# Two-layer cross-attention: the output projections of three late units dealt out in halves

## Chip, cores, metric

The kernel runs on one NeuronCore of one Trainium2 chip. The metric is the device time of the program in microseconds (us). Each time shown is one execution, and the figure compared is the median over executions.

## What is computed

Two cross-attention layers are applied in turn to 32 samples of 256 tokens with 320 channels. Each sample attends to its own 77 context rows of 512 channels, with 20 heads of 16 channels. For the inputs given, both layers reduce to the same form (the image-prompt and object branches get no context rows), everything in float32:

```
q = x @ Wq ; k = ctx @ Wk ; v = ctx @ Wv          # 20 heads of 16
p = softmax(q k^T / 4)                            # over 77 context rows
x = x + (p v) @ Wo + bo                           # output projection and residual
...
# layer 0 with its weights, then layer 1 with its own on the result
```

## The kernel before, in words

**Units.** Samples are taken in pairs: 16 pairs, two layers, so 32 *units* `(pair, layer)`, listed by `units_in_order` (L81). The last five units are `(15,0)`, `(12,1)`, `(13,1)`, `(14,1)`, `(15,1)`, with numbers 27 to 31. Units 28 to 31 are all second-layer units of four different pairs, so none of them needs what another one writes. Their results only go to memory.

**Layout.** Activations lie with channels on the 128 partitions. A unit's x, q and o are tiles of 1280 columns: two blocks of 128 channels for the two samples (512 columns each), and the last 64 channels of both samples side by side (256 columns). This gives five *groups* g = 0..4 of 256 columns, each with four pairs of heads. `of_group` (L175) cuts one out. Group 2t+b is channel block t of sample b, and group 4 is the rest.

**Steps of one unit.** Each step is a Python function that issues instructions:

- `keys`, `keys_rest` (L215, L236), `queries`, `queries_rest` (L258, L270), `vals`, `place_vals` (L284, L302): the projections on TensorE (PE), copied out by ScalarE (ACT) or VectorE (DVE), with some DMAs on the SP queue.
- `maxima(u, g)` (L319): 16 matmuls into four PSUM tiles `psm`, and four row maxima on DVE (L334).
- `turn(u)` (L341): one DVE transpose of the unit's maxima into `mT` (L343), then eight small DMAs from SP (L347) that put the maxima into spare rows of the unit's q tiles. The first four go to q tile 0, the others to q tile 1. So a unit's `scores` can start only when these have landed.
- `scores(u, g)` (L353): 16 matmuls into four `pss` tiles (L360; eight with q tile 0, then eight with q tile 1), and four exponentials on ACT (L366).
- `values(u, g)` (L409): 16 matmuls into one tile `po` (`products`, L380); a DVE transpose (L392), a reciprocal (L396) and a multiplication on GpSimd, POOL (L401).
- `turn_back(u, g)` (L412): a DVE transpose (L415) into the unit's tile `oT`, which has two buffers (L371).
- `finish(u)` (L428): the output projection of groups 0 to 3. These are 96 matmuls at L173 into four `psy` tiles: 64 from the two channel blocks, then 32 from the last channels. Four DVE additions into x follow (L422).
- `finish_rest(u)` (L436): 24 matmuls (L212) and one addition for group 4, then the DMA that stores the pair's whole x (L443). The last unit stores each group by itself (L426).

**PSUM.** All matmul outputs come from one ring of eight tiles (`bank`, L103). The n-th tile asked for reuses the (n-8)-th, so it waits until that one has been read out.

**Order.** Nothing is scheduled by a tool: the order of the program is written out by *slots*. `at(slot, where, step)` files a step, and the loop at L497 to L501 issues, slot by slot, the steps in the order load, maxima, turn, scores, values, rest, back, full, last. Every engine and every DMA queue takes its instructions in that order. With s = 5u, a unit has its queries in slot s-9, maxima in s-6 to s-2, turn in s-2, scores in s to s+4, values and turn_back one slot later. Before the change, `finish` is in s+6 and `finish_rest` in s+8. Only the two last units differ: unit 30 has both in slot 159 and unit 31 both in slot 160, the last slot. So a full slot has maxima of unit u+1, scores and values of unit u, and some projections. The slots after 153 have no maxima and no projections of a later unit left.

In the last slots before the change, PE gets this besides scores and values:

| slot | before the change |
|---|---|
| 146 | maxima, finish(28), queries(31) |
| 147, 148, 149, 150 | maxima, and keys(31); finish_rest(28) and keys_rest(31); vals; queries_rest(31) |
| 151 | maxima(31,2), finish(29) |
| 152 | maxima(31,3) |
| 153 | maxima(31,4), turn(31), finish_rest(29) |
| 154 to 158 | nothing |
| 159 | finish(30), finish_rest(30) |
| 160 | values(31,4) alone, then finish(31), finish_rest(31) |

Scores run from (30,1) in slot 151 to (31,4) in slot 159, and values one slot behind, from (30,0) in slot 151 to (31,4) in slot 160.

Of the kernel before, what the change touches and what calls it, by code (L numbers as in the profile page):

```python
# [48 lines left out]
F32 = mybir.dt.float32  # L49
# [6 lines left out]
P = 128  # L56
NB = 2
NT = NB * S
NX = 2 * NT + S
NP = B // NB  # L60
NG = 5
# [19 lines left out]
def units_in_order():  # L81
    order = [(p, 0) for p in range(AHEAD)]
    for p in range(NP):
        order.append((p, 1))
        if p + AHEAD < NP:
            order.append((p + AHEAD, 0))
    return order
# [3 lines left out]
def xattn_kernel(ctx: ExitStack, tc: tile.TileContext, xT, cT, cP, weights, outT):  # L91
    nc = tc.nc
# [3 lines left out]
    work = ctx.enter_context(tc.tile_pool(name="work", bufs=3))  # L96
# [3 lines left out]
    units = units_in_order()  # L100
    NU = len(units)

    def bank(name):  # L103
        return psum.tile([P, 512], F32, tag="bank", name=name)

    xs, cs, cvs = {}, {}, {}

    def load_x(p):
        x_sb = io.tile([P, NX], F32, tag="x", name=f"x_{p}", bufs=AHEAD + 3)
        nc.sync.dma_start(out=x_sb, in_=xT[p])  # L110
        xs[p] = x_sb

    def load_context(u):
        p = units[u][0]
        c_sb = cs[u] = io.tile([P, NKA, NB * L], F32, tag="c", name=f"c_{u}", bufs=3)
        nc.sync.dma_start(out=c_sb, in_=cP[:, p])
# [51 lines left out]
    st = [{} for _ in units]  # L168

    def by_columns(out, lhsT, rhs, **flags):  # L170

        for m in range(0, out.shape[0], 32):
            nc.tensor.matmul(out[m : m + 32], lhsT[:, m : m + 32], rhs, **flags)  # L173

    def of_group(x, g):  # L175

        if g < 4:
            return x[:, (g // 2) * NT + (g % 2) * S : (g // 2) * NT + (g % 2 + 1) * S]
        return x[:, 2 * NT : NX]

    def last_channels(ps, w2, x, **flags):
        for t in range(2):
            for b in range(NB):
                r = slice(64 * b, 64 * b + 64)
                by_columns(
                    ps[t][b][:, 0:S], w2[r, 0, t * P : (t + 1) * P], x[r, 2 * NT : NX], **flags
                )

    def main_channels(ps, w, x, start, stop):
        for t in range(2):
            for kc in range(2):
                for b in range(NB):
                    i = kc * NT + b * S
                    by_columns(
                        ps[t][b][:, 0:S], w[:, kc, t * P : (t + 1) * P], x[:, i : i + S],
                        start=(start and kc == 0), stop=(stop and kc == 1),
                    )

    def project_rest(ps, w, w22, x):

        for kc in range(3):
            for i in range(4):
                b, m = i // 2, i % 2
                r = slice(32 * i, 32 * i + 32)
                if kc < 2:
                    lhsT = w[:, kc, 2 * P + 32 * m : 2 * P + 32 * m + 32]
                    rhs = x[:, kc * NT + b * S : kc * NT + (b + 1) * S]
                else:  # L210
                    lhsT, rhs = w22[:, 0, r], x[:, 2 * NT : NX]
                nc.tensor.matmul(ps[r, 0:S], lhsT, rhs, start=(kc == 0), stop=(kc == 2))  # L212


    def keys(u):  # L215
        p, layer = units[u]
        w, c_sb = w_sb[layer], cs[u]
        kT = st[u]["k"] = work.tile([P, 2, NG, L], F32, tag="kT", name=f"kT_{u}", bufs=3)
        for t in range(2):
            ps = bank(f"psk_{u}_{t}")  # L220
            for kc in range(NKA):
                by_columns(
                    ps[:, 0 : 2 * L],
                    w["k"][:, kc, t * P : (t + 1) * P],
                    c_sb[:, kc, :],
                    start=(kc == 0),
                    stop=(kc == NKA - 1),
                )
            nc.vector.tensor_tensor(
                kT[:, :, 2 * t : 2 * t + 2].rearrange("p e g k -> p e (g k)"),  # L230
                ps[:, 0 : 2 * L].unsqueeze(1).broadcast_to([P, 2, 2 * L]),
                masks.unsqueeze(2).broadcast_to([P, 2, 2 * L]),
                ALU.mult,
            )
# [44 lines left out]
    def load_chunk(layer, i):  # L279
        n = min(P, B * L - i * P)  # L280
        c_sb = cvs[layer, i] = io.tile([P, NKA, P], F32, tag="cv", name=f"cv_{layer}_{i}", bufs=3)
        nc.sync.dma_start(out=c_sb[:, :, :n], in_=cT[:, :, i * P : i * P + n])
# [85 lines left out]
    def products(u, g):  # L368
        vpad = st[u]["v"]
        if "o" not in st[u]:  # L370
            st[u]["o"] = work.tile([P, NX], F32, tag="oT", name=f"oT_{u}", bufs=2)  # L371
        po = bank(f"po_{u}_{g}")
        pT = st[u].pop(("p", g))
        for e in range(2):
            for j in range(4):
                if g < 4:
                    b, pair = g % 2, 4 * (g // 2) + j
                else:
                    b, pair = j // 2, 8 + j % 2
                nc.tensor.matmul(  # L380
                    po[32 * j : 32 * j + 32, e * S : (e + 1) * S],
                    vpad[:L, b, pair, e].rearrange("p a d -> p (a d)"),
                    pT[j][:L, e * S : (e + 1) * S],
                    start=True,
                    stop=True,
                )
        return po
# [30 lines left out]
    def add(u, g, ps):  # L418
        p, layer = units[u]
        x = of_group(xs[p], g)  # L420
        t = g // 2
        nc.vector.scalar_tensor_tensor(  # L422
            x, ps[:, 0:S], w_sb[layer]["b"][:, 0, t : t + 1], x, ALU.add, ALU.add
        )
        if u == NU - 1:
            nc.sync.dma_start(out=of_group(outT[p], g), in_=x)  # L426

    def finish(u):  # L428
        w = w_sb[units[u][1]]
        ps = [[bank(f"psy_{u}_{t}_{b}") for b in range(NB)] for t in range(2)]  # L430
        main_channels(ps, w["o"], st[u]["o"], start=True, stop=False)
        last_channels(ps, w["o2"], st[u]["o"], start=False, stop=True)
        for g in range(4):
            add(u, g, ps[g // 2][g % 2])

    def finish_rest(u):  # L436
        p, layer = units[u]
        w = w_sb[layer]
        ps = bank(f"psy_{u}_2")
        project_rest(ps, w["o"], w["o22"], st[u]["o"])  # L440
        add(u, 4, ps)
        if layer == 1 and u < NU - 1:
            nc.sync.dma_start(out=outT[p], in_=xs[p])  # L443
        st[u].clear()


    place = {}
# [1 line left out]
    def at(slot, where, step):  # L449
        place.setdefault((slot, where), []).append(step)  # L450

    made = [0, 0]
    for u, (p, layer) in enumerate(units):
        s = NG * u
        if layer == 0 and u > 0:
            at(s - 14, "load", lambda p=p: load_x(p))
        if u > 0:
            at(s - 12, "load", lambda u=u: load_context(u))
        at(s - 8 if u else s - 9, "rest", lambda u=u: keys(u))
        at(s - 9, "last", lambda u=u: queries(u))  # L460
        at(s - 7, "rest", lambda u=u: keys_rest(u))
        need = range(p * NB * L // P, ((p + 1) * NB * L - 1) // P + 1)
        when = s - 6
        for i in need:
            if i < made[layer]:
                at(when, "full", lambda u=u, i=i: place_vals(u, i))
                continue
            at(when - 3, "load", lambda layer=layer, i=i: load_chunk(layer, i))
            at(when, "full", lambda layer=layer, i=i: vals(layer, i))
            at(when, "full", lambda u=u, i=i: place_vals(u, i))  # L470
            made[layer] += 1
            when = s - 5
        at(s - 5, "rest", lambda u=u: queries_rest(u))
        for g in range(NG):
            at(s - 6 + g, "maxima", lambda u=u, g=g: maxima(u, g))
            at(s + g, "scores", lambda u=u, g=g: scores(u, g))
            at(s + g + 1, "values", lambda u=u, g=g: values(u, g))
            at(s + g + 1, "back", lambda u=u, g=g: turn_back(u, g))
        at(s - 2, "turn", lambda u=u: turn(u))
        if u < NU - 2:  # L480
            at(s + NG + 1, "full", lambda u=u: finish(u))
            at(s + NG + 3, "rest", lambda u=u: finish_rest(u))
        else:

            slot = NG * NU - (u == NU - 2)
            at(slot, "full", lambda u=u: finish(u))
            at(slot, "last", lambda u=u: finish_rest(u))


    at(-10, "load", lambda: load_weights(0, "v", "v", nc.scalar))  # L490
# [106 lines left out]
```

## Time and profile before

| | |
|---|---|
| runs shown | 992.94, 999.02, 1000.55 us |
| median of them | 999.02 us |
| the profiled execution: its own time | 995.15 us |
| its span, first to last instruction | 993.4 us |
| mean granted TensorE clock | 0.995 |
| busy in the span: PE, DVE, ACT, POOL | 977.5, 590.9, 421.7, 182.7 us |
| one maximum on DVE (L334), mean | 466 ns, x640 |
| one exponential on ACT (L366), mean | 590 ns, x640 |
| one addition on DVE (L422), mean | 479 ns, x160 |

All views are of the one profiled execution. A PE is called busy while matmuls are in flight, so a busy share says little of how fast it works. The granted clock is what the chip allowed TensorE, as a share of full speed. The chain of waits follows the work that ended last back from the end: each piece names what the end was waiting for at that time. Times are from the span's start. "L360" is a line of the kernel, and an entry such as `psy L173` is a tile name and a line.

### The profile page before, as it was taken

What the parts mean: (1) busy time and instruction counts of PE and PEld (TensorE: products, weight loads), DVE (VectorE), ACT (ScalarE), POOL (GpSimd) and SP (SyncE); (2) the same over time, 40 slices, a digit from 0 to 9 for tenths busy, and PEclk for the clock granted to TensorE, in tenths of its full rate; (3) what the DMA queues carried; (4) which work ended last, traced back from release to release, by engine and by line L of the source; (5) the groups of instructions that cost most, each with busy time, mean ns of one, the idle gap of its engine ahead of it and who ended that gap; (6) DMA issues with size and microseconds to landing.
All of it is one profiled execution on the core that took longest, in us unless ns stands there. A gap on an engine that the chain in (4) does not pass through costs nothing.

```text
span 993.4 us, 43878 instructions
## 1 busy us (share of the span) xinstructions
PE 977.5 (98%) x19664; PEld 609.0 (61%) x19664; DVE 590.9 (59%) x1380; ACT 421.7 (42%) x905; POOL 182.7 (18%) x236
## 2 busy tenths in 40 slices
PE   7899999999999999999999999999999999999988
PEld 4566665666666666665666666666666666666644
DVE  2466555666655665655666656666556656556654
ACT  1344343454444443444444444444444534444442
POOL 2122201221202222112222112221022221122211
PEclk9999999999999999999999999999999999999989
DMA  6541222221132411223212232311323111231111
GB/s 213 177 160 37 74 79 97 70 77 62 57 122 70 132 47 60 92 80 122 71 44 85 68 123 70 122 34 53 121 80 119 50 62 54 69 107 48 58 47 54
DMA packets 53949, 83.59 MB, mean 84 GB/s; under 512 B 15556, under 2 KB 35652, under 8 KB 53762
## 3 DMA queue, kind: packets, MB, share of 16 engines
q1 hardware_dynamic: 53330, 78.96, 23.9%
q8 instruction: 154, 2.52, 1.0%
q10 hardware_dynamic: 432, 1.84, 0.5%
q14 instruction: 33, 0.27, 0.1%
HBM read 35.39 MB, written 10.49 MB: 46 GB/s over the span
## 4 chain that ended last, share of the span: by engine, by line
PE 97%; DVE 1%; DMA 1%; SPq 1%; issue 0%; POOL 0%; DVEq 0%; POOLq 0%
PE po L380 16%; PE pss L360 15%; PE psy L173 14%; PE psq L173 14%; PE psm L326 12%; PE psv L173 8%; PE psk L173 7%; PE psq L212 4%; PE psy L212 4%; PE psk L245 2%; SPq L347 1%; DVE max L334 1%; DMA w<-in_w_dram 0%; DMA q<-mT 0%; DVE mT L343 0%
## 5 line engine op out<-in xcount | busy, mean ns | idle before, releaser
L366 ACT ACTIVATE pT<-pss 77x512 f32<-77x512 f32 x640 | 326.9, 590 | 242.1 <-PE pss L360 242.1
L334 DVE TENSOR_REDUCE max<-psm 128x4 f32<-128x308 f32 x640 | 259.4, 466 | 172.1 <-PE psm L326 172.1
L401 POOL TENSOR_TENSOR normal<-turned,inv 128x256 f32<-128x256 f32 x160 | 99.3, 621 | 763.9 <-DVE inv L396 763.9
L360 PE MATMUL pss<-q,kM 32*77 32x256 f32 x2560 | 180.6, 380 | 5.8 <-DMA q<-mT 5.8
L380 PE MATMUL po<-pT,v 77*32 77x256 f32 x2560 | 174.0, 389 | 1.0 <-DVE max L334 1.0
L173 PE MATMUL psy<-oT,w 128*32 128x256 f32 (+1 forms) x3072 | 149.4, 380 | 0.0
L173 PE MATMUL psq<-x,w 128*32 128x256 f32 (+1 forms) x3072 | 149.4, 380 | 0.0
L392 DVE STREAM_TRANSPOSE turned<-po 128x512 f32<-128x512 f32 x160 | 113.3, 708 | 46.0 <-PE po L380 42.9
L268 ACT COPY q<-psq 128x256 f32<-128x256 f32 x128 | 47.6, 372 | 213.3 <-PE psq L173 209.5
L326 PE MATMUL psm<-kT,q 32*128 32x154 f32 x2560 | 129.1, 314 | 0.0
L360 PEld LDWEIGHTS pss<-q,kM 32*77 32x77 f32 x2560 | 114.4, 142 | 23.4 <-issue 10.6
L326 PEld LDWEIGHTS psm<-kT,q 32*128 32x128 f32 x2560 | 91.9, 183 | 55.3 <-issue 41.7
L380 PEld LDWEIGHTS po<-pT,v 77*32 77x32 f32 x2560 | 67.5, 110 | 90.3 <-DVE max L334 58.4
L415 DVE STREAM_TRANSPOSE oT<-normal 128x256 f32<-128x256 f32 x160 | 70.9, 443 | 84.5 <-POOL normal L401 81.4
L173 PEld LDWEIGHTS psq<-x,w 128*32 128x32 f32 (+1 forms) x3072 | 85.4, 109 | 57.6 <-issue 14.4
L173 PEld LDWEIGHTS psy<-oT,w 128*32 128x32 f32 (+1 forms) x3072 | 82.2, 108 | 61.2 <-issue 13.2
L422 DVE SCALAR_TENSOR_TENSOR x<-psy,w,x 128x256 f32<-128x256 f32 x160 | 68.6, 479 | 62.8 <-PE psy L173 56.4
L173 PE MATMUL psv<-w,cv 128*32 128x320 f32 x1232 | 93.5, 433 | 0.0
L256 POOL TENSOR_SCALAR kM<-kT,less 128x385 f32<-128x385 f32 x64 | 79.9, 1260 | 38.8 <-ACT kT L253 38.6
L173 PE MATMUL psk<-c,w 128*32 128x154 f32 x2048 | 75.2, 299 | 5.6 <-DMA w<-in_w_dram 5.6
L173 PEld LDWEIGHTS psk<-c,w 128*32 128x32 f32 x2048 | 67.0, 112 | 12.8 <-DMA w<-in_w_dram 5.6
L173 PEld LDWEIGHTS psv<-w,cv 128*32 128x32 f32 x1232 | 41.0, 110 | 40.6 <-issue 1.9
(24 smaller groups left out, 328.3 us busy)
## 6 DMA issues: line engine op xcount, KB each, us to landing
q<-q SPq DMA_DIRECT2D x32, 640.0 KB
x<-in_xT_dram SPq DMA_DIRECT2D x16, 640.0 KB
c<-in_cP_dram SPq DMA_DIRECT2D x32, 308.0 KB
cv<-in_cT_dram SPq DMA_DIRECT2D x38, 256.0 KB
out_dram<-x SPq DMA_DIRECT2D x15, 640.0 KB
v<-stage SPq DMA_DIRECT2D x26, 192.5 KB
q<-mT SPq DMA_DIRECT2D x256, 5.0 KB
w<-in_w_dram ACTq DMA_DIRECT2D x2, 640.0 KB
```

The costliest lines, as they stand in the source:

```text
L173: nc.tensor.matmul(out[m : m + 32], lhsT[:, m : m + 32], rhs, **flags)
L212: nc.tensor.matmul(ps[r, 0:S], lhsT, rhs, start=(kc == 0), stop=(kc == 2))
L256: nc.gpsimd.tensor_scalar_add(kM[:, e], kT[:, e], less[:, e : e + 1])
L326: nc.tensor.matmul(ps[j][:, c * 2 * L : (c + 1) * 2 * L], q[r, c * P : (c + 1) * P], kT[r, :, g, :], start=True, stop=True,)
L334: nc.vector.tensor_reduce(mx[:, 2 * g : 2 * g + 2, 2 * j : 2 * j + 2], ps[j][:, : 4 * L].rearrange("p (c e k) -> p c e k", e=2, k=L), AX.X ...
L360: nc.tensor.matmul(ps[j][:L, e * S : (e + 1) * S], kM[r, e, g, :], q[r, :], start=True, stop=True,)
L366: nc.scalar.activation(st[u]["p", g][j][:L], ps[j][:L], AF.Exp, scale=SCALE)
L380: nc.tensor.matmul(po[32 * j : 32 * j + 32, e * S : (e + 1) * S], vpad[:L, b, pair, e].rearrange("p a d -> p (a d)"), pT[j][:L, e * S : (e ...
L392: nc.vector.transpose(turned[:, 0 : 2 * S], po)
L401: nc.gpsimd.tensor_tensor(normal.rearrange("p q e d -> p e q d"), outs, inv.unsqueeze(3).broadcast_to([P, 2, S // 32, HD]), ALU.mult,)
L415: nc.vector.transpose(of_group(st[u]["o"], g), normal)
L422: nc.vector.scalar_tensor_tensor(x, ps[:, 0:S], w_sb[layer]["b"][:, 0, t : t + 1], x, ALU.add, ALU.add)
```

## The change

Units 28, 29 and 30 (`late`) get their output projections placed by a table: the slots of the first half (channel block t = 0), of the second half (t = 1), and of `finish_rest`. With `end` = 160 these are 151, 152, 148 for unit 28; 153, 154, 155 for unit 29; and 156, 159, 157 for unit 30. `finish` can do one half: 48 matmuls into two `psy` tiles and two additions. The store becomes a step of its own, filed as the last step of the latest of the three slots: 152, 155 and 159. Unit 31 and all units up to 27 stay where they were. The tile `oT` gets a third buffer.

```
--- before.py
+++ after.py
@@ -180,16 +180,16 @@
 
 
 
-    def last_channels(ps, w2, x, **flags):
-        for t in range(2):
+    def last_channels(ps, w2, x, ts=(0, 1), **flags):
+        for t in ts:
             for b in range(NB):
                 r = slice(64 * b, 64 * b + 64)
                 by_columns(
                     ps[t][b][:, 0:S], w2[r, 0, t * P : (t + 1) * P], x[r, 2 * NT : NX], **flags
                 )
 
-    def main_channels(ps, w, x, start, stop):
-        for t in range(2):
+    def main_channels(ps, w, x, start, stop, ts=(0, 1)):
+        for t in ts:
             for kc in range(2):
                 for b in range(NB):
                     i = kc * NT + b * S
@@ -368,7 +368,7 @@
     def products(u, g):
         vpad = st[u]["v"]
         if "o" not in st[u]:
-            st[u]["o"] = work.tile([P, NX], F32, tag="oT", name=f"oT_{u}", bufs=2)
+            st[u]["o"] = work.tile([P, NX], F32, tag="oT", name=f"oT_{u}", bufs=3)
         po = bank(f"po_{u}_{g}")
         pT = st[u].pop(("p", g))
         for e in range(2):
@@ -425,13 +425,21 @@
         if u == NU - 1:
             nc.sync.dma_start(out=of_group(outT[p], g), in_=x)
 
-    def finish(u):
+    def finish(u, ts=(0, 1)):
+
         w = w_sb[units[u][1]]
-        ps = [[bank(f"psy_{u}_{t}_{b}") for b in range(NB)] for t in range(2)]
-        main_channels(ps, w["o"], st[u]["o"], start=True, stop=False)
-        last_channels(ps, w["o2"], st[u]["o"], start=False, stop=True)
-        for g in range(4):
-            add(u, g, ps[g // 2][g % 2])
+        ps = {t: [bank(f"psy_{u}_{t}_{b}") for b in range(NB)] for t in ts}
+        main_channels(ps, w["o"], st[u]["o"], start=True, stop=False, ts=ts)
+        last_channels(ps, w["o2"], st[u]["o"], start=False, stop=True, ts=ts)
+        for t in ts:
+            for b in range(NB):
+                add(u, 2 * t + b, ps[t][b])
+
+    def store(u):
+        p, layer = units[u]
+        if layer == 1 and u < NU - 1:
+            nc.sync.dma_start(out=outT[p], in_=xs[p])
+        st[u].clear()
 
     def finish_rest(u):
         p, layer = units[u]
@@ -439,9 +447,8 @@
         ps = bank(f"psy_{u}_2")
         project_rest(ps, w["o"], w["o22"], st[u]["o"])
         add(u, 4, ps)
-        if layer == 1 and u < NU - 1:
-            nc.sync.dma_start(out=outT[p], in_=xs[p])
-        st[u].clear()
+        if u not in late:
+            store(u)
 
 
     place = {}
@@ -449,6 +456,14 @@
     def at(slot, where, step):
         place.setdefault((slot, where), []).append(step)
 
+
+
+    end = NG * NU
+    late = {
+        NU - 4: (end - 9, end - 8, end - 12),
+        NU - 3: (end - 7, end - 6, end - 5),
+        NU - 2: (end - 4, end - 1, end - 3),
+    }
     made = [0, 0]
     for u, (p, layer) in enumerate(units):
         s = NG * u
@@ -477,14 +492,17 @@
             at(s + g + 1, "values", lambda u=u, g=g: values(u, g))
             at(s + g + 1, "back", lambda u=u, g=g: turn_back(u, g))
         at(s - 2, "turn", lambda u=u: turn(u))
-        if u < NU - 2:
+        if u == NU - 1:
+            at(s + NG, "full", lambda u=u: finish(u))
+            at(s + NG, "last", lambda u=u: finish_rest(u))
+            continue
+        at(late[u][2] if u in late else s + NG + 3, "rest", lambda u=u: finish_rest(u))
+        if u not in late:
             at(s + NG + 1, "full", lambda u=u: finish(u))
-            at(s + NG + 3, "rest", lambda u=u: finish_rest(u))
-        else:
-
-            slot = NG * NU - (u == NU - 2)
-            at(slot, "full", lambda u=u: finish(u))
-            at(slot, "last", lambda u=u: finish_rest(u))
+            continue
+        for t in range(2):
+            at(late[u][t], "full", lambda u=u, t=t: finish(u, (t,)))
+        at(max(late[u]), "last", lambda u=u: store(u))
 
 
     at(-10, "load", lambda: load_weights(0, "v", "v", nc.scalar))
```

## The prediction

> **What bounds the kernel now.** I read the page first, then the windows, the chain of waits, PE's waits, and the DVE timeline.
>
> ```profile
> PE 977.5 (98%) x19664; PEld 609.0 (61%) x19664; DVE 590.9 (59%) x1380; ACT 421.7 (42%) x905; POOL 182.7 (18%) x236
> PEclk9999999999999999999999999999999999999989
> ```
>
> PE is busy for 98% of the span, and the clock row falls in one place, the last slice but one. So nothing but PE matters in the middle, and the end has something of its own. The windows cut it out (columns: PE, PEld, DVE, ACT, POOL busy; clock; DMA share; GB/s):
>
> ```profile
> 58.00:944.00 886.00, 885.77 (x18006) 556.88 (x18004) 543.06 (x1267) 387.24 (x834) 166.71 (x208) 1.00 0.24 79
> 944.00:963.00 19.00, 15.49 (x265) 8.66 (x260) 11.25 (x27) 7.40 (x15) 2.48 (x4) 0.99 0.11 40
> 963.00:973.00 10.00, 10.00 (x88) 3.57 (x80) 2.83 (x6) 5.70 (x12) 1.24 (x2) 0.51 0.08 31
> 973.00:994.00 21.00, 17.02 (x324) 9.10 (x320) 9.71 (x22) 4.50 (x9) 2.48 (x4) 0.98 0.18 64
> ```
>
> From 58 to 944 us PE idles 0.23 us in all. From 944 to 963 it idles 3.5 us. Then for 10 us it is "busy" at half the clock: 88 matmuls, where 10 us in the middle hold about 203. The chain of waits (start, length, what) gives the pieces:
>
> ```profile
> 944.15 4.48 PE psy L173 x96
> 948.63 0.74 PE psm L326 x16
> 949.37 1.67 PE pss L360 x16
> 951.04 1.04 PE po L380 x16
> ...
> 955.91 0.52 DVE mT L343
> ...
> 960.65 1.66 DMA q<-mT
> 962.31 0.24 issue
> 962.55 1.15 PE pss L360 x8
> 963.70 1.87 PE po L380 x16
> 965.57 1.94 PE pss L360 x16
> ...
> 976.14 1.19 PE po L380 x16
> 977.33 4.48 PE psy L173 x96
> ```
>
> The first piece is finish(29), slot 151. The chain leaves PE in slot 153: the last maxima, the transpose mT, eight DMA issues, their landing at 962.31, and only then the second half of scores(31,0). Pieces of 0.86 (pss) and 1.00 (po) at full clock take 1.94 and 1.87 afterwards. PE's own waits confirm the gaps:
>
> ```profile
> PE pss L360 <- DMA q<-mT: 2.7, 2, 1.7
> PE po L380 <- DVE max L334: 0.8, 1, 0.8
> ```
>
> So the end is bound by two waits and a clock drop, with finish(30) (4.48 + 1.43 us) standing behind them where it covers nothing.
>
> **What the Trainium skill says.** "TensorE: Matmul & The Clock Gate", Part 1, says that TensorE's clock is either full or half, set by how busy the PE was in free-running windows of about 3.4 us, and that a busy window restores it. The trace agrees: 0.50 in the two-us windows from 964 to 972, 1.00 from 973, and the drop follows 2.7 us of idling within 959.2 to 962.6. "DMA: Bandwidth & Descriptors", Anatomy of one DMA, gives about 2 us of fixed cost per DMA; here the last 5 KB transfer landed 1.66 us after its issue. The same page, Queues, rings and completion order, says that each DMA engine consumes descriptors in ring order; nothing in this trace tests that for a store ahead of a turn.
>
> **The work at full speed.** The chain from 944.15 to the end of the last L212 matmuls at 990.06 lasts 45.91 us. At full-clock prices from the same chain its PE work is: finish(29) 4.48; maxima 2 x 0.74 = 1.48; scores (30,2) to (31,4), 8 x 0.86 = 6.88; values (30,1) to (31,4), 9 x 1.00 = 9.00; finish_rest(29) 1.30; finish and rest of 30 and of 31, 2 x 5.78 = 11.56. Sum 34.70. So 11.2 us are lost: idling 3.5 (0.81 + 0.98 + 1.72); half clock 5.4 (excess over full price of the six pieces from 962.55 to 973.07: 0.72 + 0.87 + 1.08 + 0.86 + 1.08 + 0.77); 0.8 in scores(30,2), which waited for finish(29)'s third and fourth additions to free PSUM tiles; the rest, 1.5, in small pieces.
>
> **The change part by part.**
>
> *Slot 146 loses finish(28): 4.48 us of PE earlier.* queries(31) then follows po at once, at 914.57. Its first PSUM tiles are psm tiles whose maxima end at 914.33, and one exponentiated by then: no wait. Its ACT copies came 2.4 us after its first matmul; the exponentials ahead of them end at 915.66, before 916.9. Slots 147 to 150 move up by 4.48; the chunk needed in slot 149 is issued at 913.27 and used at 935.5, so 17 us remain. Cost nothing.
>
> *The same matmuls come back in slots 151 and 152; no instruction is added.* 48 matmuls take 2.24 us, two additions about 0.42 each back to back (1.66 for four). Slots 151, 152, 153, 154, 156 and 159 get a half, 155 and 157 a rest of 1.30. Per slot PE then has 0.74 + 0.86 + 1.00 + 2.24 = 4.84 us to 153, 4.10 or 3.16 to 157, and 1.86 in 158. ACT needs 2.04 for four exponentials, so it is covered except in slot 158: values(31,3) follows its scores by 1.00 + 0.86 against 0.1 + 2.04, a wait of 0.3 (before, the same place cost 0.19).
>
> *DVE and the ring in slots 151 to 153.* DVE has four maxima 1.62, the transpose of po to the end of turn_back 2.3 (POOL in between), two additions 0.83: 4.75 of 4.84. In slot 152 scores take their third and fourth PSUM tiles from the two psy tiles of slot 151. With T the end of those matmuls, the additions end near T + 0.55 and T + 1.0, and the tiles are wanted at T + 0.96 and T + 1.07. That is a tie. Bounds: 0, or 0.81 as four additions cost before; I take 0.3 in slot 152 and 0.3 in 153.
>
> *turn(31).* With slot 151 starting at 937.07 (4.48 earlier), slot 153's maxima end on DVE at about 949.6 and mT at 950.1 (two additions are ahead of them, 0.8 us). Before, mT ended at 956.43 and the second half of scores(31,0) started 6.1 us later. So q tile 1 is ready at 956.2, q tile 0 about 2.4 earlier. PE's own work brings it to the second half at 956.2 without ring stalls and 956.8 with them: finish(29) in two halves is the cover, 4.48 us instead of a rest of 1.30. Margin 0 to 0.6 us; the wait of 2.7 and the clock drop behind it go. If the cover fails, each us late costs one us, and the clock is next.
>
> *Stores.* On SP, store(28) now stands ahead of the eight issues. It waits for its addition until about 948, takes 0.39 to issue, and a 640 KB store is done about 2.6 us after issue (store(29), issued 961.29; the DMA rate is 0 from 964). So it is gone near 951; the issues start at 950.1, and the last four near 952.5. Covered; at worst the first four land a us later, where q tile 0 has 2 us. store(29) in 155 and store(30) in 159 are behind all turns.
>
> *Third oT buffer.* oT of unit 30 first asks for a buffer in slot 151; with two it would be unit 28's, now read until 152. With three nothing waits. No instruction; no cost.
>
> *Tail.* Slot 160 and the output DMAs are as before.
>
> Sum: 11.2 recovered, less 0.6 (ring), 0.3 (slot 158), 0.2 (ends of L212 groups, 1.48 against 1.30): 10.1 us. The profiled execution's 995.15 becomes 985.0 (span 983.3). The three runs and it have the middle (995.15 + 999.02) / 2 = 997.1, which I take as the base: 997.1 - 10.1 = **987**.
>
> **Rivals.**
>
> *More ring stalls (0.18).* DVE at 4.75 of 4.84 us slips, and slots 152 to 154 each lose 0.81 instead of two losing 0.3: 1.8 more, 988.8. For it: scores(30,2) did so. Against: two additions, not four.
>
> *The turn is still late (0.10).* mT slips behind the additions, PE idles 2.7 and the clock halves as before (5.4): of 10.1, 2.0 is left, 995.1. Against: 3.2 us more cover.
>
> *The clock drop is not in the usual execution (0.10).* It hangs on a free-running window, and the lowest run is 2.2 below the profiled one. Then 10.1 - 5.4 = 4.7: 992.4. Against: that run is faster by less than the drop costs. The same doubt can help: 999.02 may hold a longer drop, and the gain would be up to 14.
>
> *Slower (0.02).* The store ahead of the turn holds its transfers: below about 0.6 us nothing is lost, then each us is one, and the clock's 5.4 returns. It passes 999.02 once the hold is over 0.6 + (999.0 - 987.0) - 5.4 = 7.2 us, and is 1% slower (1009) at 17 us; a store takes 2.6.
>
> **How the numbers follow.** The forecast has 0.60, with 983 to 991 as its own range, since the runs differ by 7.6 us. Lowest run less 10 to 14 is 979 to 983; the late turn and the missing drop reach 995 and 992. Range 979 to 994. One per cent, about what a measurement can tell here, is 10 us, so below 989.0 counts as faster against 999.02. Faster: 0.50 of the forecast, 0.10 of the ring case: 0.60. Same: 0.10 + 0.08 + 0.10 + 0.10 = 0.38. Slower 0.02.
>
> **What would show it.** Clock 1.00 in every window from 58 us to the end; PE's waits for q<-mT gone after 100 us; psy L173 in groups of 48; scores in slots 152 and 153 at 0.9 to 1.2 us; the last L212 ending near 980. A clock below 0.9 there, or a wait for q<-mT over 1 us, would make it wrong; so would idling between 914 and 937, where slot 146 lost its filler.

## The result, and the profile after

The changed kernel takes 987.82 us (median of 6 runs, 987.63 to 988.27), beside 995.13 us for the kernel before in the same comparison (6 runs, 992.84 to 1000.55). The ratio is 0.9913, with an interval of 0.9888 to 0.9937. A second comparison gave 988.07 against 997.36 us, ratio 0.9911 (0.9890 to 0.9931). The profiled execution took 987.73 us, with a span of 985.9 us, 7.5 us less than before.

The page of the kernel after, sections 1 and 2:

```profile
PE 973.4 (99%) x19664; PEld 608.9 (62%) x19664; DVE 591.6 (60%) x1380; ACT 421.7 (43%) x905; POOL 182.7 (19%) x236
PEclk9999999999999999999999999999999999999999
```

The instruction counts of all engines are those of before; only the order has changed. The one low digit in the clock row is gone. The windows of the kernel after (same columns as before):

```profile
944.00:963.00 19.00, 19.00 (x337) 10.05 (x338) 12.26 (x28) 8.64 (x17) 2.48 (x4) 1.00 0.12 43
963.00:973.00 10.00, 10.00 (x181) 5.09 (x174) 5.16 (x11) 6.40 (x14) 1.86 (x3) 1.00 0.15 60
```

From 944 to 963 us PE held 265 matmuls and 15.5 busy us before, and holds 337 and 19.0 now. From 963 to 973 it runs at clock 1.00, not 0.51, and does 181 instead of 88. PE has no idle time to speak of from 900 us to its last matmul at 982.6 (82.59 of 82.60 us busy). PE's waits over the whole span:

```profile
PE psk L173 <- DMA c<-in_cP_dram: 5.8, 1, 5.8
PE pss L360 <- DMA q<-mT: 3.1, 2, 1.6
PE po L380 <- DVE max L334: 0.2, 1, 0.2
```

The waits for the turn (`q<-mT`) were 5.8 us in four places. The two that are left lie in the first 41 us, outside the change. The chain of waits of the kernel after never leaves PE in its last 82 us:

```profile
940.65 2.32 PE psy L173 x48
942.97 0.74 PE psm L326 x16
943.71 1.32 PE pss L360 x16
945.03 1.00 PE po L380 x16
...
949.09 1.32 PE pss L360 x16
...
951.41 2.32 PE psy L173 x48
953.73 1.03 PE pss L360 x16
...
972.17 1.19 PE po L380 x16
973.36 2.32 PE psy L173 x48
975.68 1.00 PE po L380 x16
976.68 4.48 PE psy L173 x96
981.16 1.48 PE psy L212 x24
```

The pieces `x48` are halves; there are six of them, three of which are shown. (The trace shows a float32 matmul of the program as two records, so `x48` is 24 instructions; the counts of matmuls ahead of this section are counts of records.) Two things cost more than the prediction priced them at: the halves take 2.32 us, and scores take 1.32 in slots 152 and 153 and 1.03 in the slots without maxima.

### The profile page after: what moved, and what is told of

Same layout as the page of the kernel before. It is cut to its first block, busy times and chain, and to the rows that moved or that the text cites. A ratio compares the mean times of both kernels' runs of the same rounds, so it can differ in the third digit from the quotient of the medians.

```text
span 985.9 us, 43879 instructions
## 1 busy us (share of the span) xinstructions
PE 973.4 (99%) x19664; PEld 608.9 (62%) x19664; DVE 591.6 (60%) x1380; ACT 421.7 (43%) x905; POOL 182.7 (19%) x236
## 4 chain that ended last, share of the span: by engine, by line
PE 98%; DVE 1%; DMA 1%; SPq 0%; issue 0%; POOL 0%; POOLq 0%
PE po L380 16%; PE pss L360 15%; PE psq L173 15%; PE psy L173 15%; PE psm L326 12%; PE psv L173 9%; PE psk L173 7%; PE psq L212 4%; PE psy L212 4%; PE psk L245 2%; DMA c<-in_cP_dram 1%; SPq L347 0%; DVE max L334 0%; DMA q<-mT 0%; DVE mT L343 0%
## 5 line engine op out<-in xcount | busy, mean ns | idle before, releaser
L360 PE MATMUL pss<-q,kM 32*77 32x256 f32 x2560 | 177.9, 376 | 3.1 <-DMA q<-mT 3.1
L380 PE MATMUL po<-pT,v 77*32 77x256 f32 x2560 | 171.5, 385 | 0.2 <-DVE max L334 0.2
```

The source lines that it names most:

```text
L360: nc.tensor.matmul(ps[j][:L, e * S : (e + 1) * S], kM[r, e, g, :], q[r, :], start=True, stop=True,)
L380: nc.tensor.matmul(po[32 * j : 32 * j + 32, e * S : (e + 1) * S], vpad[:L, b, pair, e].rearrange("p a d -> p (a d)"), pT[j][:L, e * S : (e ...
```

## The experiments

My theory: idling before scores(31,0), while the turn's transfers are under way, takes the clock down. What pays is useful PE work behind the turn's transpose. Rivals: the thin slots 155 to 158 take the clock down, so that all nine slots have to be filled; the third buffer; or luck in a kernel whose runs spread over 7 us.

| kernel | median us (runs) | spread us | ratio to before, interval |
|---|---|---|---|
| third buffer alone | 998.33 (14) | 993.15 to 1000.59 | 1.0003 (0.9985 to 1.0021) |
| idle matmuls, 6.05 us | 994.64 (18) | 993.99 to 995.49 | 0.9972 (0.9960 to 0.9983) |
| idle matmuls, 3.02 us | 992.19 (6) | 991.60 to 992.43 | 0.9952 (0.9933 to 0.9971) |
| no cover at the turn | 993.31 (8) | 992.76 to 994.36 | 0.9959 (0.9941 to 0.9976) |
| half the cover | 989.09 (6) | 988.49 to 989.69 | 0.9922 (0.9903 to 0.9941) |
| only unit 28 moved | 988.37 (4) | 987.82 to 988.66 | 0.9907 (0.9880 to 0.9935) |
| whole finishes | 989.62 (6) | 989.49 to 990.26 | 0.9928 (0.9910 to 0.9947) |
| the change again | 988.07 (6) | 987.43 to 988.32 | 0.9911 (0.9890 to 0.9931) |
| the change, and queries(2) moved | 984.35 (5) | 984.23 to 985.25 | 0.9874 (0.9851 to 0.9897) |

The kernel before had medians of 998.93 (35 runs), 997.36 (11) and 997.52 us (9) beside these. Since its own spread is large, kernels without a clock drop are better compared with each other by their medians.

**The third buffer alone.**

```
-            ... tag="oT", name=f"oT_{u}", bufs=2)
+            ... tag="oT", name=f"oT_{u}", bufs=3)
```

> The kernel before with a third oT buffer and nothing else. Theory (the third buffer is only a permission; the spread of the kernel before comes from its clock drop in the last slices): median 995 us as before, within 3 us, runs spread over 5 to 8 us, and the mean clock of a run falls as its time rises: 0.995 near 995, about 0.990 near 1000, 0.998 or more near 993. Rival 1 (the buffer itself removes a wait): faster by over 3 us. Rival 2 (the spread comes from the start, from loading): times differ by 5 us or more at one and the same clock.

No change: 1.0003, with a median of 998.33 us, which is 3.3 above the 995 expected; the kernel before had 998.93 beside it. The second part of the expectation held, but for the fastest runs, at 0.997 and not 0.998. The 35 runs of the kernel before that stood beside it have mean clocks that go with their times: 993.2 to 993.5 us at 0.997 (4 runs), 995.5 to 996.0 at 0.995 (4), 997.1 to 997.3 at 0.993 (3), 997.5 to 999.4 at 0.991 and 0.990 (20), 1000.6 at 0.988 (1). One group is out of order: three runs of 994.3 at 0.994. This profiled execution took 999.46 us, and its windows show where the time went:

```profile
944.00:964.00 20.00, 16.48 (x285) 9.05 (x280) 12.53 (x30) 8.19 (x16) 2.48 (x4) 1.00 0.13 48
964.00:982.00 18.00, 18.00 (x168) 7.36 (x168) 6.63 (x14) 10.23 (x20) 2.48 (x5) 0.54 0.07 25
```

The same program idles 3.5 us up to 964 as in the first profile. Then it runs at half clock for some 17 us, up to the dense finish(30), instead of 10. Going by the clocks of the 35 runs (0.990 or 0.991 in 20 of them, 0.995 in the execution that I predicted from), the usual execution of the kernel before has this longer drop.

**Idle matmuls before scores(31,0).** No useful work moves; PE gets extra matmuls whose result nobody reads.

```
+    def idle_work(n):
+        ps = bank("psz")
+        for i in range(n):
+            by_columns(ps[:, 0:S], w_sb[1]["o"][:, 0, 0:P], xs[NP - 1][:, 0:S], start=True, stop=True)
...
+    at(NG * NU - 5, "maxima", lambda: idle_work(14))
```

> The kernel before with 56 extra matmuls of 256 columns, whose result nobody reads, placed in slot 155 just before scores(31,0), where the PE waits for the turn; no useful work is moved. They take about 2.6 us. Theory (idling while the turn is on its way takes the clock down, and the half clock costs 5.4 us): the clock stays at 1.00 to the end, and the time is about 990 us with a spread under 2 us, though PE has more to do. Rival (the clock falls because slots 155 to 158 are thin): the drop stays, and the time is 995 or more.

I had sized it wrong: 56 instructions are 112 records and took 6.05 us, 3.4 more than the wait, so 990 us could not come out. Even so the time fell, to 994.64 us with a spread of 1.5 us, and the clock stayed at 0.998 or more in every run. I halved it (`idle_work(7)`):

> The kernel before with idle matmuls before scores(31,0), now half as many as in dummy_before_scores (28 instructions, 56 in the trace, about 3.0 us, no longer than the wait for the turn). No useful work is moved, their result is not read. Theory (the clock falls because PE idles there): the clock stays up, 991 us (994.6 less the 3.05 us of matmuls taken out), spread under 2 us. Rival (it takes more than 3 us of work to hold the clock): the drop comes back in some runs, spread over 4 us.

992.19 us, 1.2 above the number expected, with a spread of 0.8 us and clocks of 0.997 to 1.000. (A run's mean clock counts half clock outside the end's work too: in the profiled execution at the first turn, shown below, and from 989.4 us, after PE's last matmul, where it costs nothing.) The chain of waits of this kernel:

```profile
960.28 3.02 PE psz L173 x56
963.30 1.03 PE pss L360 x16
964.34 1.00 PE po L380 x16
965.34 1.03 PE pss L360 x16
966.37 1.19 PE po L380 x16
```

With 3 us of useless work in the wait, the thin slots behind run at full clock: 1.03 and 1.00 to 1.19 us, not 1.94 and 1.87. In these runs thinness does not take the clock down; idling does. Against the 997.36 of the kernel before this is worth 5.2 us; putting useful work there instead gives another 4.1 (992.19 to 988.07).

**No cover, half a cover.** Both keep the halves, the stores and the order of the DMA queue; pieces of unit 29 move to behind the wait, and its store with the last of them.

```
-        NU - 3: (end - 7, end - 6, end - 5),
+        NU - 3: (end - 5, end - 3, end - 2),
```

That is the kernel without cover at the turn. The one with half the cover has `(end - 7, end - 5, end - 2)` in that place.

> The changed kernel with the two halves of unit 29 moved from slots 153 and 154, behind the turn's transpose, to slots 155 and 157, and its rest from 155 to 158: all pieces still dealt out in halves, the same queues, but no cover for the turn. Theory (what pays is cover for the turn's DMAs, and the clock goes with it): PE idles about 3.5 us before scores(31,0), the clock falls to half for some us although the slots behind are now full, and the time is 992 to 996 us. Rival (full slots behind keep the clock up): 3.5 us lost, 991 us. Rival (dealing out as such pays, wherever the pieces are): 988 us.

993.31 us, in the theory's range, 5.2 to 5.5 us above the change. The timeline of PE in this kernel at scores(31,0) (start, length, operation, and in brackets the idle time before it):

```profile
955.18 0.67 PE L360 MATMUL pss<-q,kM 32*77 32x256 f32 x8 [1.67 <-DMA q<-mT]
957.58 1.03 PE L360 MATMUL pss<-q,kM 32*77 32x256 f32 x8 [1.73 <-DMA q<-mT]
```

And its windows behind that place:

```profile
957.50:961.00 3.50, 3.42 (x32) 1.44 (x36) 0.46 (x1) 2.05 (x4) 0.00 (x0) 0.54 0.03 5
961.00:992.00 31.00, 26.82 (x500) 13.61 (x492) 14.65 (x33) 8.18 (x16) 3.73 (x6) 1.00 0.18 65
```

The idle time is 3.4 us where 3.5 was expected, and the clock fell. But it was back after 3.4 us, where the kernel before took 10 to 17: full slots behind do not prevent the drop, they shorten it. So that rival had a part of the truth. (Two of the eight runs, at 0.995 and 0.994, must have had more half clock than this one at 0.997.)

> The changed kernel with only one half of unit 29 as cover for the turn (slot 153); its second half goes from slot 154 to 155 and its rest to 158. In the changed kernel PE comes to the second half of scores(31,0) 1.1 us after the turn's transfers are there, so with 2.3 us less cover it waits 1.2 us. Theory (a wait this short does not take the clock down): clock 0.998 or more, 989.0 us, spread under 1.5 us. Rival (any wait there takes it down): 990.5 to 993 us and clocks of 0.997 and less.

989.09 us, and the clock is 0.998 to 1.000 in all runs. The timeline of PE in this kernel, at the second half of scores(31,0):

```profile
957.40 0.67 PE L360 MATMUL pss<-q,kM 32*77 32x256 f32 x8 [1.13 <-DMA q<-mT]
```

The wait is 1.13 us. So 1.1 us of idling there costs 1.0 us and no clock. In the kernel before, 2.7 us of idling at this place brought the drop. But the length of a wait does not decide by itself. At the first turn PE waits about 1.49 and 1.60 us in every kernel here but the last, with 0.67 us of matmuls between, and there the clock fell in six of the ten profiled executions that have this wait. Here are half the cover, where it fell, and the change, where it did not (the clock is the third number from the end):

```profile
31.00:41.00 10.00, 6.91 (x124) 3.68 (x124) 5.30 (x13) 1.57 (x5) 2.50 (x2) 0.92 0.12 35
31.00:41.00 10.00, 6.91 (x148) 4.06 (x140) 6.21 (x16) 0.97 (x3) 2.50 (x2) 1.00 0.14 48
```

The drops follow a fixed beat. Read in windows of 0.1 us, they last 3.41 us (all six at the first turn, and the one without cover), 10.24 us (the kernel before) and 17.07 us (third buffer alone): one, three and five times 3.41. Where one execution has two, they start 269.0 such periods apart (39.58 and 957.76 us, no cover) and 271.0 (40.29 and 965.30 us, third buffer). So it is the idling within one period that seems to count. In the period just before each of these nine drops PE idled 1.7 to 2.7 us; the kernel before, whose beat splits the first turn's wait into 1.5 and 1.6 us in two periods, had no drop there. This is worked out from traces taken for other questions; no run tested it by itself.

**Only unit 28 moved.** Units 29 and 30 are where the kernel before has them.

```
+        NU - 4: (end - 8, end - 6, end - 12),
+        NU - 3: (end - 9, end - 9, end - 7),
+        NU - 2: (end - 1, end - 1, end - 1),
...
+        if late[u][0] == late[u][1]:
+            at(late[u][0], "full", lambda u=u: finish(u))
```

> Only unit 28 is moved, its halves to slots 152 and 154; units 29 and 30 stay where the kernel before has them (slots 151 and 153; slot 159), so slots 155 to 158 have nothing but scores and values. Theory (cover up to slot 154 is what pays): clock 1.00 to the end, idling under 1 us, 0.8 us for ring waits in slot 152, time 988 to 990 us. Rival (all nine slots have to be filled): the clock falls again or each thin slot loses over 0.5 us, 992 us or more.

988.37 us: all of the gain but 0.3 to 0.6 us, with one of the three units. The chain shows the cost of thin slots 155 to 158 at full clock:

```profile
960.46 1.00 PE po L380 x16
...
962.50 1.16 PE po L380 x16
```

About 0.16 us in every second slot, where values wait for the exponentials. Dealing out over nine slots is not what gives most of the gain.

**Whole finishes.** All three units moved, but in one piece each (slots 151, 153, 156).

> The three moved projections whole instead of in halves: unit 28 in slot 151, 29 in 153, 30 in 156, the rests as in the change (148, 155, 157). The cover behind the turn's transpose is the same 4.5 us. Theory: 0.5 us saved on halves (2.32 against 2.24 each), 0.35 lost on a longer wait for additions in slot 152 and about 1 us because slot 152 has only 2.6 us of PE work against 4 us of DVE work: 988.5 to 989.5 us, clock up. Rival (halves make no difference): 987.3 to 987.8. Rival (whole pieces bring the clock drop back): over 990.

989.62 us, 1.6 above the change and 0.1 above the range expected; the clock stays up (0.998 or more). Slot 152 without a half pays about as priced: in its chain scores took 1.67 us against 1.32, and then PE waited 0.8 us for a maximum before the `po` of slot 153. What I had left out is slot 159, which now has nothing to cover the last exponentials (the last two `po` pieces together take 3.01 us, about one more than at 1.00 each).

**The change again**, for the comparison with these:

> The changed kernel once more, beside the kernels of this call. Theory: 987.8 us with a spread under 1.5 us and a clock of 0.998 to 1.000 in every run, against a kernel before that spreads over 7 us; ratio to it 0.988 to 0.992. Rival (the gain of the first comparison was luck in the runs of before): ratio above 0.994.

As expected: 988.07 us, spread 0.9 us, every clock 0.998 or 1.000.

**The same cure at the start.** The two waits left in PE's list are those of the first unit's turn.

```
-        at(s - 9, "last", lambda u=u: queries(u))
+        at(s - 9 if u != 2 else -1, "last", lambda u=u: queries(u))
```

> The changed kernel, and the same cure at the other end: queries(2) goes from slot 1 to slot -1, behind the first turn's transpose, where PE in the profile waits 3.1 us for the first unit's turn (PE's waits, q<-mT, about 40 us into the span). Theory (useful PE work behind a turn is worth the wait it covers): that wait goes, 4.6 us of work are covered, 985 us, 2.5 to 3.1 us below the changed kernel, clock up. Rival (x of pair 2 or a PSUM tile is not there yet so early, or ACT, which then copies the queries before the first exponentials, becomes the wait): 987.5 us or more.

984.35 us, 3.7 below the change: the fastest version here, ratio 0.9874 (0.9851 to 0.9897). The whole list of PE's waits in this kernel:

```profile
PE psk L173 <- DMA w<-in_w_dram: 5.7, 1, 5.7
PE po L380 <- DVE max L334: 1.0, 2, 0.8
```

The waits for `q<-mT` are gone, and PE waits 1.0 us for maxima, not 0.2. Its window at the first turn:

```profile
31.00:41.00 10.00, 10.00 (x224) 5.84 (x216) 4.41 (x12) 2.46 (x7) 2.50 (x2) 1.00 0.10 25
```

That window held 148 matmuls and 3.1 us of idling in the changed kernel, and holds 224 and none here. But the move does not explain all of the 3.7 us. The two profiled executions (984.34 and 987.73 us) differ by 3.4. From the projection ahead of the first turn (33.71 us in the change, 32.76 here) to the next one (61.39 and 58.04), this kernel gains 2.4 us: 3.1 of idling less some 0.75 of new waiting for a maximum. The other 0.95 us were there before the moved work, from a quicker start of that execution. Between the medians there is also half clock: four of the six runs of the change show 0.998, and all five here 1.000. And the two medians are of different comparisons. In the traced pair the move itself is worth 2.4 us, a little under the 2.5 to 3.1 expected.

## Why the prediction came out as it did

The mechanism was right: the end was bound by the wait for the turn and the half clock behind it, and the work put there removed both. The sum for the profiled pair was 10.1 us; measured to the end of the last L212 matmuls it is 7.4. By its terms:

| term of the sum, us | predicted | measured |
|---|---|---|
| idling and half clock removed, with all small pieces | 11.2 | 11.2 |
| slots 152 and 153, additions and PSUM tiles | -0.6 | -0.92 (2 x 0.46) |
| slot 159 ("slot 158" in the prediction), values(31,3) waiting for exponentials | -0.3 | -0.19 |
| end of the last L212 group | -0.2 | -0.18 |
| six halves at 2.32, not 2.24 | 0 | -0.48 |
| six scores without maxima ahead, 1.03, not 0.86 | 0 | -1.02 |
| slot 151 starts 3.50 us earlier, not 4.48 | 0 | -0.98 |
| sum | 10.1 | 7.4 |

- **The term that was mis-sized is "scores (30,2) to (31,4), 8 x 0.86".** 0.86 is the least price of scores right behind maxima. Behind psy or po they cost 1.03, and the kernel before had shown it, in scores(30,4) at 957.07 and, after the drop, from 973.07 us:

```profile
942.29 0.86 PE pss L360 x16
...
973.07 1.03 PE pss L360 x16
```

So 0.86 stood in the chain ahead of the stretch that was priced, not in it. The halves' 0.08 may be of the same kind: a half goes once more from matmuls of 128 rows to matmuls of 64. The Trainium skill, "TensorEngine Tiling (Array Packing)", Tiling Modes, says that changing the tiling mode drains the TensorE. The trace fits: maxima and scores both use 32 rows (`32*128`, `32*77`), psy and po 128 and 77. That the drain is the cause was not tested by itself.
- **Slot 146 "cost nothing": nearly right.** queries(31) followed po at once, but took 4.62 us against 4.45, so the slot cost 0.17. The other 0.81 of the missing 0.98 us was there before the change begins: finish_rest of slot 143 starts at 899.89 us, against 899.08, most of it (0.68 by 61 us) from a slower start of that execution.
- **The ring tie in slots 152 and 153** went to the wait: 0.46 each, inside the bounds of 0 and 0.81.
- **The turn.** mT ended at 951.35 us, not 950.1 (0.98 of it is the late slot 151). Scores(31,0) were not held up, and the margin was 1.1 us, not 0 to 0.6; half the cover showed it by waiting 1.13 us for an expected 1.2.
- **Stores.** store(28) was issued at 949.30, ahead of the turn's eight issues from 951.43, and nothing shows that it held them up. With half the cover, where PE waits for the turn behind such a store, the second half of scores(31,0) starts 6.07 us after the first issue; it was 6.05 us in the kernel before, without one.
- **The base.** I took 997.1 us. The kernel before has medians of 995.1 to 998.9, depending on how many of its runs have the long drop. My rival that the drop might be missing in the usual execution is refuted: each of its 55 runs in the later comparisons has a clock of 0.997 or less, where half clock at the first turn alone leaves 0.998, and the median one has more of it than the profile.
- **Luck.** That 987.0 lies 0.8 us below the result is in part luck. In the first comparison the base was 2.0 too high (997.1 for 995.13) and the gain 2.8 too large (10.1 for 7.3), and the two nearly cancel. The sum itself gave 985.0 for the profiled execution, and the changed one took 987.73. To carry the 10.1 over to a slower base was not sound: as the clocks of the later runs show, a slower run of the kernel before has a longer drop, and a kernel without the drop does not inherit it.
- **The signs.** Clock 1.00 from 58 us on, no wait for `q<-mT` after 100 us, groups of 48 and no idling from 914 to 937 us came as written. Scores in slots 152 and 153 took 1.32 us, outside the 0.9 to 1.2 named, and the last L212 ended at 982.6, not near 980.
- **The chances.** I gave "faster by over 1%" 0.60. Both intervals, 0.9888 to 0.9937 and 0.9890 to 0.9931, span 0.99. A single percentage cannot be given, since the kernel before has none: its time is a range of 7 us, and the changed one's of 0.9.

## What to carry to other kernels

When TensorE is busy throughout, look for the places where it waits for a round trip (here eight DMA issues and their landing, 6.1 us from the end of the transpose) and keep back work that nobody is waiting for, to put it right behind the start of the trip; it need not be spread further than the wait. Read the clock in narrow windows: 2.7 us of waiting cost 5.4 us more at half clock in the profiled execution, and more than that in the usual one. And price an instruction group by what will stand ahead of it, not by what it took elsewhere.

## What the runs showed of the hardware

- Useless matmuls in a wait made the kernel faster by 5 us (997.36 to 992.19), by keeping the clock up.
- A drop lasted 3.4 us before dense work, and 10.2 and 17.1 us before slots of 2 us of PE work each: one, three and five times 3.41 us. In one execution the drops start whole multiples of that apart.
- At the first turn the same wait of 3.1 us in two pieces took the clock down in six executions and not in four; 1.1 us at the end brought no drop in six runs.
- A kernel whose runs spread over 7 us became one that spreads over 0.9 us when the drop was gone: most of that spread was the length of the drop (clocks of 0.997 at 993 us to 0.988 at 1001 us).
